# Attention values for two query halves at once, equal score pieces, and two-bank maxima

## The chip, the cores and the metric

The program runs on one core of a Trainium2 chip. The metric is the device time of one execution in microseconds (us), the median of the runs shown. TensorE (PE) multiplies, VectorE (DVE) reduces and adds, ScalarE (ACT) takes exponentials and copies, GpSimd (POOL) does small elementwise work, and SyncE (SP) issues DMAs. PEld is the weight load of TensorE, which runs beside its matmuls.

## The reference

Four layers, each a cross-attention and a feed-forward network, with the residual added around both; `x` is 8 batches of 256 tokens by 128, and the context is 8 batches of 1601 rows by 64.

```python
x = x + xattn0(layernorm(x), ctx)   # 16 heads of 8
x = x + ffn0(layernorm(x))
x = x + xattn1(layernorm(x), ctx)   # 16 heads of 64
x = x + ffn1(layernorm(x))
x = x + xattn2(layernorm(x), ctx)   # 1 head of 64
x = x + ffn2(layernorm(x))          # experts
x = x + xattn3(layernorm(x), ctx)   # 16 heads of 8
x = x + ffn3(layernorm(x))          # experts
# xattn: softmax(q k^T * scale, over 1601 keys) v, then an output product
```

## The kernel before, in words

Everything is fp32. The scheduler is told to keep the order in which the program issues (`manual_schedule`), so the order of the calls in the loops is the order in each engine's queue. PSUM, the memory that matmuls write, has eight banks of 512 columns; a stage divides them by name, as in `psum(s=4, t=2, o=1, m=1)`. A tile of a name can be written again only when the readers of the one before it in the same bank are done.

**`wide`, attentions 1 and 2.** The unit of work is a job: one batch, one head, and one half `j` of 128 queries. Attention 1 has 8 x 16 x 2 = 256 jobs, attention 2 has 16. A job holds queries on partitions and keys along the row. Its steps, with the lines that the profile names:

- `scores` (L467): four tiles `st` of 512, 512, 512 and 66 columns, each by two matmuls (the high and the low part of the queries).
- `maximum` (L474 for a tile, L477 over the four): DVE.
- `exponentials` (L488): ACT, from the score tiles into `e`, with row sums.
- `turn` (L500, copy at L502): thirteen transposes of 128 keys by PE into four `t` tiles, which ACT (the first two) and DVE (the last two) copy to `pt`.
- `values` (L514): 13 chunks of keys; even chunks write partitions 0 to 63 of the single `o` tile, odd ones 64 to 127, so that two matmuls of 64 columns of weights run side by side. They are 128 queries wide.
- `sums` (L519, L520) on DVE; `take` (L524), a copy of `o` by ACT; `project` (L528), a matmul with the output weights into the free half of `o`; `add` (L532), by DVE, to the residual.
- `query` (L438, L443, L444): once for two jobs, the queries of a later head.

The loop of job n issues: scores and maxima of n+1; turns 0 and 1 of n; project and add of n-1; the query; exponentials of n+1; turns 2 and 3 and sums of n; then values and take of n. Steps of the feed-forward networks 0 and 1, of the query weights and of the next stage are run beside the jobs by `run(beside[n], EARLY)` and `run(beside[n], LATE)`, before and after the values.

**`narrow`, attentions 0 and 3.** A unit is one batch and a group of four heads: 32 units. Keys are on partitions here, so that no transposes are needed, and the maxima are computed first, by matmuls of their own. A unit has seven steps of two chunks of 128 keys, each in two half steps t, one for each pair of heads. A half step issues: `score(p, t)` (L1069, two `st` tiles, and L1072, their exponentials on ACT); `values` (L1081) of one chunk of the step before; what is due of `beside` (keys L777, values L834, context chunks L761, queries L814, the row flip L808, the output product L913); and what is due of `tasks`: a `pair` of maxima (L873, two matmuls of 512 columns into two `pm` tiles, and L876, one DVE reduction of each) for a unit ahead, or `shift` (L882 and on), which follows the last of them. `place_shift` (L895, L897) puts the maxima into the queries. `plan` gives each `pair` a due half step, spread over a unit's fourteen, and `DONE` is the half step by which they end. The end of a unit copies the `ov` tile (L1085). Tiles: `psum(m=3, s=4, o=1)`. `bank()` hands out `st` tiles for the scores and for the work beside them. The placed keys and queries are kept for `RING = 4` units.

Of the kernel before, what the change touches and what calls it, by code (L numbers as in the profile page):

```python
# [39 lines left out]
P = 128  # L40
# [9 lines left out]
TAKEN = -3.0e38  # L50
KW = LK + 1
RING = 4
DONE = 8
AFTER = 26


# [1 line left out]
def decoder_kernel(ctx: ExitStack, tc: tile.TileContext, a: dict, out: bass.AP):  # L58
# [331 lines left out]
    def wide(layers, before, extra):  # L390
# [11 lines left out]
        with ExitStack() as es:  # L402
# [54 lines left out]
            jobs = [(k, h, j) for k in keys for h in range(layers[k[0]][0]) for j in range(QT)]  # L457
            st, e, ls, tail = {}, {}, {}, {}

            BANK = [(at, min(512, LK - at)) for at in range(0, LK, 512)]  # L460

            def scores(n, c):
                k, h, j = jobs[n]
                st[n, c] = ps["s"].tile([P, 512], F32, tag="s", name="st")
                at, w = 512 * c, min(512, KW - 512 * c)
                for i in range(2):
                    nc.tensor.matmul(st[n, c][:, 0:w], lhsT=q[k, h][i][:, j * P:(j + 1) * P],  # L467
                                     rhs=ct[k][:, at:at + w], start=(i == 0), stop=(i == 1))

            def maximum(n, c):  # L470

                if c == 0:
                    ls[n] = two.tile([P, 12], F32, tag="ls", name="ls", bufs=3)
                nc.vector.tensor_reduce(ls[n][:, c:c + 1], st[n, c][:, 0:BANK[c][1]], AX.X, ALU.max)  # L474
                if c == 3:
                    shift = ls[n][:, 4:5]
                    nc.vector.tensor_reduce(shift, ls[n][:, 0:4], AX.X, ALU.max, negate=True)  # L477
# [14 lines left out]

            def turn(n, i):

                t = ps["t"].tile([P, 512], F32, tag="t", name="t")
                p = turned[n, i] = two.tile([P, 512], F32, tag="pt", name="pt", bufs=5)
                cs = range(4 * i, min(4 * i + 4, NC))
                m = P if cs[-1] < NC - 1 else LAST
                for c in cs:
                    nc.tensor.transpose(t[0:m, (c - 4 * i) * P:(c - 4 * i + 1) * P], e[n][:, c * P:c * P + m], ident)  # L500
                w = P * len(cs)
                (nc.scalar.copy if i < 2 else nc.vector.tensor_copy)(p[0:m, 0:w], t[0:m, 0:w])  # L502

            o = {}

            def values(n, cs):

                k, h, j = jobs[n]
                if cs[0] == 0:
                    o[n] = po()  # L510
                for c in cs:
                    m = P if c < NC - 1 else LAST
                    half = slice(DC * (c % 2), DC * (c % 2) + DC)
                    nc.tensor.matmul(o[n][half, 0:P], lhsT=v[k][0:m, c, :],  # L514
                                     rhs=turned[n, c // 4][0:m, (c % 4) * P:(c % 4 + 1) * P],
                                     start=(c < 2), stop=(c >= NC - 2))
# [5 lines left out]
            def take(n):  # L522
                tail[n] = two.tile([P, P], F32, tag="os", name="os")
                nc.scalar.copy(tail[n], o[n][:, 0:P])  # L524

            def project(n):
                (l, _), h, j = jobs[n]
                nc.tensor.matmul(o[n][:, P:P + D], lhsT=tail[n], rhs=B[l][:, h, :], start=True, stop=True)  # L528

            def add(n):  # L530
                (_, b), h, j = jobs[n]
                nc.vector.scalar_tensor_tensor(X[b][:, j, :], o[n][:, P:P + D], ls[n][:, 9:10], X[b][:, j, :],  # L532
                                               ALU.mult, ALU.add)

            last = len(jobs) - 1

            loads, measures, starts, turns, ahead = {}, {}, {}, {}, {}
            for n, (k, h, j) in enumerate(jobs):
# [28 lines left out]
            for n, (_, h, j) in enumerate(jobs):  # L567
                more = n < last
                for k in loads.get(n, []):
                    load_batch(k)  # L570
                if more:
                    for c in range(4):
                        scores(n + 1, c)
                        maximum(n + 1, c)
                turn(n, 0)
                turn(n, 1)
                if n:
                    project(n - 1)
                    add(n - 1)
                for k in measures.get(n, []):  # L580
                    measure(k)
                for k in starts.get(n, []):
                    start_batch(k)
                for k in turns.get(n, []):
                    turn_y(k)

                at = n + 2 if n + 2 == first_of_last else n + 3
                if (j == 1 and n + 3 != first_of_last or at == first_of_last != n + 3) and at <= last:
                    for f in query(*jobs[at][0:2]):
                        f()  # L590
                if more:
                    exponentials(n + 1)
                turn(n, 2)
                turn(n, 3)
                sums(n)
                run(beside.get(n, []), EARLY)
                values(n, range(NC))
                take(n)
                run(beside.get(n, []), LATE)
            project(last)  # L600
            add(last)

    def maps1(two, A, B):

# [69 lines left out]
    def narrow(wq, wkT, wvT, wo, bq, bk, bv, bo, first, after=None, last=None):  # L674
# [8 lines left out]
        with ExitStack() as es:  # L683
            one = es.enter_context(tc.tile_pool(name="na1", bufs=1))
            two = es.enter_context(tc.tile_pool(name="na2", bufs=2))
            es.enter_context(psum(m=3, s=4, o=1))
            es.enter_context(tc.manual_schedule())

            def bank():
# [172 lines left out]
            def maxima(n):  # L862
# [3 lines left out]

                def pair(t, js, at, w):
                    k, q = K[n % RING][t], Q[n % RING][t]
                    pt = [pm() for g in range(2)]
                    for x, j in enumerate(js):  # L870
                        for g in range(2):
                            r = slice(64 * g, 64 * g + 64)
                            nc.tensor.matmul(pt[g][:, x * w:(x + 1) * w], lhsT=q[r, j * P:(j + 1) * P],  # L873
                                             rhs=k[r, at:at + w], start=True, stop=True)
                    for g in range(2):
                        nc.vector.tensor_reduce(mx[:, js[0]:js[-1] + 1, 2 * t + g, at // 512],  # L876
                                                pt[g][:, 0:len(js) * w].rearrange("p (j k) -> p j k", k=w),
                                                AX.X, ALU.max)

                def shift():  # L880
# [140 lines left out]
            for n in range(units):  # L1021
# [67 lines left out]

                for p in range(steps):  # L1090
                    e = two.tile([P, 4, 2, LQ], F32, tag="e", name="e")
                    for t in range(2):
                        score(p, t, e)
                        if n == p == 0:
                            spare(6)
                        if before:
                            before.pop(0)()
                        while beside and (beside[0][0] * 2 * steps < 2 * p + t + 1 or p * t == steps - 1):
                            beside.pop(0)[1]()
                        for f in tasks.pop(per * n + 2 * p + t, []):  # L1100
                            f()
                    before = [lambda c=c, e=e, values=values: values(c, e)
                              for c in range(2 * p, min(2 * p + 2, NC))]
            *inverses, project = finish(NB - 1)
# [292 lines left out]
    def ffn1(p, b):  # L1397
# [42 lines left out]

        def up(i):
            if i == 0:
                t["h"] = p.tile([P, 4, LQ], F32, name="f1_h")
# [45 lines left out]

        def take_r(j):  # L1490
            if j == 0:
                t["rT"] = p.tile([P, QT, 512], F32R, name="f1_rT")
# [441 lines left out]
```

## Time and profile before

| | us |
|---|---|
| runs | 3539.5, 3535.34, 3530.77 |
| median of the runs | 3535.34 |
| span of the profiled execution | 3529.4 |
| attention 0 | 55 to 708.5 |
| attention 1 | 737.5 to 2323 |
| attention 2 | 2323 to 2459 |
| experts of layer 2 | 2459 to 2685 |
| attention 3 | 2685 to 3318.7 |
| experts of layer 3 and output | 3318.7 to 3529.4 |

The profile is of one execution. Its page gives each engine's busy time, share of the span and number of instructions. A table by stretches gives the same by stage. The timeline lists instructions, or runs of like ones, with start, length, engine, line, operation, output and input tiles with their shapes, and, in brackets, the idle time before it with what ended it.

### The profile page before, as it was taken

Reading aid. Unit: us, or ns where it says so; the run is one execution under the profiler, and the core shown is the slowest. Engines: PE = TensorE matmul, PEld = TensorE weight load, DVE = VectorE, ACT = ScalarE, POOL = GpSimd, SP = SyncE. Lnnn points to the kernel's source line nnn. Section 1 sums busy time; section 2 is a strip of 40 time slices with the busy share of each in tenths; the row PEclk is TensorE's granted clock in tenths of the full one; section 3 lists DMA queues with packets and bytes.
Section 4 is the critical chain, followed back from the end, with each engine's and each line's share of the span. In section 5 each row is a group of like instructions: output and inputs, shape, how many; then the busy total and the mean of one; then the engine's idle time right before and its main releaser. Section 6 shows DMA issues by size and latency. Waiting matters only on the chain.

```text
span 3529.4 us, 75160 instructions
## 1 busy us (share of the span) xinstructions
PE 3380.6 (96%) x28453; PEld 2299.7 (65%) x28453; DVE 2580.6 (73%) x6482; ACT 2290.0 (65%) x5747; POOL 1179.4 (33%) x2105
## 2 busy tenths in 40 slices
PE   7999999989999999999999999988999999999999
PEld 4555555468787877788787878866445555555444
DVE  6888888656776767676776767675557888888665
ACT  3888887746666666667666666654224878787622
POOL 6344344624152513324151520131115333332100
PEclk8999999989999999999999999999998999999999
DMA  5544444120001001000100000021004444443100
GB/s 97 89 73 74 71 77 58 19 83 1 15 1 33 2 1 39 1 15 1 39 1 22 6 1 15 1 66 33 1 0 85 78 63 68 65 69 53 41 5 7
DMA packets 113449, 130.24 MB, mean 37 GB/s; under 512 B 67616, under 2 KB 96832, under 8 KB 112448
## 3 DMA queue, kind: packets, MB, share of 16 engines
q1 hardware_dynamic: 92352, 114.22, 18.0%
q0 software_dynamic: 20480, 10.53, 1.3%
q8 instruction: 225, 3.69, 0.4%
q10 hardware_dynamic: 256, 0.69, 0.1%
q14 instruction: 136, 1.11, 0.1%
HBM read 44.79 MB, written 11.28 MB: 16 GB/s over the span
## 4 chain that ended last, share of the span: by engine, by line
PE 81%; DVE 9%; ACT 6%; POOL 2%; issue 2%; DMA 0%; DVEq 0%; POOLq 0%; SPq 0%; ACTq 0%
PE ov L1081 13%; PE o L514 12%; PE st L467 12%; PE pm L873 11%; PE t L500 8%; PE st L1069 6%; PE gu L1740 3%; PE o L1789 3%; PE gu L1741 3%; ACT pt L502 3%; DVE ls L474 2%; DVE mx L876 2%; ACT e L488 2%; PE st L834 1%; DVE ql L444 1%
## 5 line engine op out<-in xcount | busy, mean ns | idle before, releaser
L876 DVE TENSOR_REDUCE mx<-pm 128x1 f32<-128x512 f32 (+1 forms) x1792 | 1020.3, 627 | 172.7 <-PE pm L873 168.9
L1072 ACT ACTIVATE e<-st 128x512 f32<-128x512 f32 (+1 forms) x1792 | 910.6, 566 | 210.5 <-PE st L1069 160.0
L474 DVE TENSOR_REDUCE ls<-st 128x1 f32<-128x512 f32 x1088 | 549.5, 567 | 292.3 <-PE st L467 291.2
L488 ACT ACTIVATE e<-st,ls 128x512 f32<-128x512 f32 x1088 | 634.0, 602 | 13.4 <-DVE ls L477 12.6
L502 ACT COPY pt<-t 128x512 f32<-128x512 f32 x544 | 293.6, 586 | 460.8 <-PE t L500 459.9
L1081 PE MATMUL ov<-e,V 128*32 128x256 f32 x6656 | 564.6, 392 | 0.3 <-ACT e L1072 0.3
L873 PE MATMUL pm<-K,Q 64*128 64x512 f32 (+1 forms) x2048 | 497.3, 451 | 18.6 <-DVE mx L876 15.4
L500 PE MATMUL t<-ident,e 128*128 128x128 f32 (+1 forms) x3536 | 506.5, 281 | 2.6
L514 PE MATMUL o<-pt,v 128*64 128x128 f32 (+1 forms) x7072 | 490.2, 278 | 17.0 <-DVE pt L502 13.0
L514 PEld LDWEIGHTS o<-pt,v 128*64 128x64 f32 (+1 forms) x7072 | 412.1, 137 | 88.2 <-DVE pt L502 37.2
L873 PEld LDWEIGHTS pm<-K,Q 64*128 64x128 f32 x2048 | 226.1, 187 | 325.8 <-DVE mx L876 223.3
L500 PEld LDWEIGHTS t<-ident,e 128*128 128x128 f32 (+1 forms) x3536 | 391.5, 141 | 52.4 <-ACT pt L502 30.0
L467 PE MATMUL st<-ct,qh 128*128 128x512 f32 x1088 | 406.1, 373 | 1.8 <-ACT e L488 1.8
L1069 PE MATMUL st<-Q,K 64*128 64x256 f32 (+1 forms) x3328 | 403.1, 287 | 0.1
L467 PE MATMUL st<-ct,ql 128*128 128x512 f32 x1088 | 362.9, 367 | 0.0
L1069 PEld LDWEIGHTS st<-Q,K 64*128 64x128 f32 (+1 forms) x3328 | 333.1, 182 | 32.3 <-issue 6.5
L855 POOL DMA_DIRECT2D Q<-qh x256 | 128.3, 501 | 450.5 <-PE st L1069 422.9
L502 DVE COPY pt<-t 128x512 f32<-128x512 f32 (+1 forms) x544 | 239.1, 481 | 34.9 <-PE t L500 34.8
L467 PEld LDWEIGHTS st<-ct,qh 128*128 128x128 f32 x1088 | 205.6, 189 | 86.3 <-issue 34.9
L1081 PEld LDWEIGHTS ov<-e,V 128*32 128x32 f32 x6656 | 142.5, 108 | 153.7 <-issue 37.9
L1742 ACT ACTIVATE act<-gu 128x512 f32<-128x512 f32 x130 | 77.5, 597 | 243.2 <-PE gu L1741 232.1
L488 ACT ACTIVATION_READ_ACCUMULATOR e<-st,ls 128x1 f32 x1088 | 230.7, 212 | 0.0
(545 smaller groups left out, 4302.2 us busy)
## 6 DMA issues: line engine op xcount, KB each, us to landing
K<-kh SPq DMA_DIRECT2D x250, 100.1 KB
K<-kl SPq DMA_DIRECT2D x250, 100.1 KB
ct<-ctd SPq DMA_DIRECT2D x23, 801.0 KB
ctd<-ct SPq DMA_DIRECT2D x8, 801.0 KB
v<-in_ctx SPq DMA_DIRECT2D x16, 384.0 KB
Q<-qh POOLq DMA_DIRECT2D x256, 16.0 KB, 2.7
Q<-ql POOLq DMA_DIRECT2D x256, 16.0 KB, 3.0
raw<-in_ctx SPq DMA_DIRECT2D x8, 384.0 KB
```

The lines of the kernel that those rows point to most:

```text
L467: nc.tensor.matmul(st[n, c][:, 0:w], lhsT=q[k, h][i][:, j * P:(j + 1) * P], rhs=ct[k][:, at:at + w], start=(i == 0), stop=(i == 1))
L474: nc.vector.tensor_reduce(ls[n][:, c:c + 1], st[n, c][:, 0:BANK[c][1]], AX.X, ALU.max)
L488: nc.scalar.activation(e[n][:, at:at + w], st[n, c][:, 0:w], AF.Exp, bias=ls[n][:, 4:5], scale=1.0, accum_out=ls[n][:, 5 + c:6 + c])
L500: nc.tensor.transpose(t[0:m, (c - 4 * i) * P:(c - 4 * i + 1) * P], e[n][:, c * P:c * P + m], ident)
L502: (nc.scalar.copy if i < 2 else nc.vector.tensor_copy)(p[0:m, 0:w], t[0:m, 0:w])
L514: nc.tensor.matmul(o[n][half, 0:P], lhsT=v[k][0:m, c, :], rhs=turned[n, c // 4][0:m, (c % 4) * P:(c % 4 + 1) * P], start=(c < 2), stop=(c ...
L855: nc.gpsimd.dma_start(out=q[r:P:8, :].bitcast(F32), in_=qhl[b][r % 2][src, :].bitcast(F32))
L873: nc.tensor.matmul(pt[g][:, x * w:(x + 1) * w], lhsT=q[r, j * P:(j + 1) * P], rhs=k[r, at:at + w], start=True, stop=True)
L876: nc.vector.tensor_reduce(mx[:, js[0]:js[-1] + 1, 2 * t + g, at // 512], pt[g][:, 0:len(js) * w].rearrange("p (j k) -> p j k", k=w), AX.X, ...
L1069: nc.tensor.matmul(st[g][0:m, j, :], lhsT=k[r, c * P:c * P + m], rhs=q[r, :], start=True, stop=True)
L1072: nc.scalar.activation(e[0:m, 2 * t + g, 0:len(cs), :], st[g][0:m, 0:len(cs), :], AF.Exp)
L1081: nc.tensor.matmul(cell["o"][32 * g:32 * g + 32, :], lhsT=v[0:m, at:at + 32], rhs=e[0:m, g, c % 2, :], start=(c == 0), stop=(c == NC - 1))
```

## The change

In `wide`, the scores are cut into four nearly equal pieces (400, 400, 400 and 401 columns, the last multiplied as 402). The turned tiles of both jobs of a pair (one batch and head, both query halves) share one `pt` buffer, and `values` multiplies a chunk for both halves at once, 256 wide; the last chunk, of 65 keys, is two matmuls of 128. In attention 1 these values are those of the pair before, half of the chunks in each job, issued after the exponentials of n+1 and before turn 2. `take` follows in the odd job, and `project` with its two adds comes at the head of the next even job, ahead of turn 0. In attention 2 the values of both jobs are issued at the odd one. In `narrow`, a pair of maxima writes one tile of two banks, which one reduction reads; scores have three banks instead of four; and a step issues the first score, the maxima due in both half steps, the second score, the work beside, and then both chunks of values. `DONE` goes from 8 to 6. Two tiles of feed-forward network 1 share a buffer.

```diff
-DONE = 8
+DONE = 6
...
-            BANK = [(at, min(512, LK - at)) for at in range(0, LK, 512)]
+            BANK = [(400 * c, 400 if c < 3 else LK - 1200) for c in range(4)]
...
-                at, w = 512 * c, min(512, KW - 512 * c)
+                at, w = BANK[c]
+                w += w % 2
...
-                    ls[n] = two.tile([P, 12], F32, tag="ls", name="ls", bufs=3)
+                    ls[n] = two.tile([P, 12], F32, tag="ls", name="ls", bufs=8)
...
-                p = turned[n, i] = two.tile([P, 512], F32, tag="pt", name="pt", bufs=5)
+                if j == 0:
+                    turned[p, i] = two.tile([P, len(cs), QT, P], F32, tag="pt" if i < 3 else "pt3", name="pt",
+                                            bufs=5 if i < 3 else 2)
...
+            HALVES = (0, 1, 2, 3, 4, 5), (6, 7, 8, 9, NC - 1, 10, 11)
...
+            def values(p, cs):
+
+                k, h, _ = jobs[QT * p]
                 if cs[0] == 0:
+                    o[p] = po()
                 for c in cs:
+                    if c == NC - 1:
+                        for j in range(QT):
+                            nc.tensor.matmul(o[p][DC * j:DC * j + DC, j * P:(j + 1) * P], lhsT=v[k][0:LAST, c, :],
+                                             rhs=turned[p, c // 4][0:LAST, 0, j, :], start=False, stop=False)
+                    else:
+                        half = slice(DC * (c % 2), DC * (c % 2) + DC)
+                        nc.tensor.matmul(o[p][half, 0:LQ], lhsT=v[k][:, c, :],
+                                         rhs=turned[p, c // 4][:, c % 4, :, :].rearrange("p j q -> p (j q)"),
+                                         start=(c < 2), stop=(c >= NC - 3))
...
+            def project(p):
+                (l, b), h, _ = jobs[QT * p]
+                for j in range(QT):
+                    nc.tensor.matmul(o[p][:, LQ + j * P:LQ + j * P + D], lhsT=tail[p][:, j * P:(j + 1) * P],
+                                     rhs=B[l][:, h, :], start=True, stop=True)
+                for j in range(QT):
+                    nc.vector.scalar_tensor_tensor(X[b][:, j, :], o[p][:, LQ + j * P:LQ + j * P + D],
+                                                   ls[QT * p + j][:, 9:10], X[b][:, j, :], ALU.mult, ALU.add)
...
+            now = layers[0][0] * NB - 1
...
+                p = n // QT
+                if j == 0 and 2 <= p <= now:
+                    project(p - 2)
                 turn(n, 0)
                 turn(n, 1)
-                if n:
-                    project(n - 1)
-                    add(n - 1)
+                if j == 0 and p > now:
+                    project(p - 1)
...
                 if more:
                     exponentials(n + 1)
+                if 1 <= p <= now:
+                    values(p - 1, HALVES[j])
+                    if j == 1:
+                        take(p - 1)
+                        if p == now:
+                            project(p - 1)
                 turn(n, 2)
                 turn(n, 3)
                 sums(n)
                 run(beside.get(n, []), EARLY)
-                values(n, range(NC))
-                take(n)
+                if p >= now and j == 1:
+                    values(p, HALVES[0] + HALVES[1])
+                    take(p)
                 run(beside.get(n, []), LATE)
...
-            es.enter_context(psum(m=3, s=4, o=1))
+            es.enter_context(psum(mm=2, s=3, o=1))
...
-                    pt = [pm() for g in range(2)]
+                    pt = ps["mm"].tile([P, 2, 512], F32, tag="mm", name="pm")
...
+                    to = mx[:, js[0]:js[-1] + 1, 2 * t:2 * t + 2, at // 512]
+                    if len(js) == 1:
+                        nc.vector.tensor_reduce(to[:, 0, :], pt[:, :, 0:w], AX.X, ALU.max)
...
+                    score(p, 0, e)
                     for t in range(2):
-                        score(p, t, e)
-                        if n == p == 0:
-                            spare(6)
-                        if before:
-                            before.pop(0)()
-                        while beside and (beside[0][0] * 2 * steps < 2 * p + t + 1 or p * t == steps - 1):
-                            beside.pop(0)[1]()
                         for f in tasks.pop(per * n + 2 * p + t, []):
                             f()
+                    score(p, 1, e)
+                    if n == p == 0:
+                        spare(6)
+                    while beside and (beside[0][0] * 2 * steps < 2 * p + 2 or p == steps - 1):
+                        beside.pop(0)[1]()
+                    for f in before:
+                        f()
```

More of the change, by code (lines that the diff above doesn't have):

```diff
@@ L493, in turn @@
             def turn(n, i):
+                p, j = divmod(n, QT)
+                cs = range(4 * i, min(4 * i + 4, NC))
                 t = ps["t"].tile([P, 512], F32, tag="t", name="t")
-                p = turned[n, i] = two.tile([P, 512], F32, tag="pt", name="pt", bufs=5)
-                cs = range(4 * i, min(4 * i + 4, NC))
+                if j == 0:
+                    turned[p, i] = two.tile([P, len(cs), QT, P], F32, tag="pt" if i < 3 else "pt3", name="pt",
+                                            bufs=5 if i < 3 else 2)
                 m = P if cs[-1] < NC - 1 else LAST
@@ L500, in turn @@
                     nc.tensor.transpose(t[0:m, (c - 4 * i) * P:(c - 4 * i + 1) * P], e[n][:, c * P:c * P + m], ident)
-                w = P * len(cs)
-                (nc.scalar.copy if i < 2 else nc.vector.tensor_copy)(p[0:m, 0:w], t[0:m, 0:w])
+                (nc.scalar.copy if i < 2 else nc.vector.tensor_copy)(
+                    turned[p, i][0:m, :, j, :], t[0:m, 0:P * len(cs)].rearrange("p (c q) -> p c q", q=P))
             o = {}
-            def values(n, cs):
-                k, h, j = jobs[n]
+            HALVES = (0, 1, 2, 3, 4, 5), (6, 7, 8, 9, NC - 1, 10, 11)
+            def values(p, cs):
+                k, h, _ = jobs[QT * p]
                 if cs[0] == 0:
-                    o[n] = po()
+                    o[p] = po()
                 for c in cs:
[L512 to L516, printed above, removed]
+                    if c == NC - 1:
[7 more added lines that the diff above has]
+                                         start=(c < 2), stop=(c >= NC - 3))
             def sums(n):
@@ L520, in sums, with take @@
                 nc.vector.reciprocal(ls[n][:, 9:10], ls[n][:, 9:10])
[L522 to L533, printed above, removed]
+            def take(p):
+                tail[p] = two.tile([P, LQ], F32, tag="os", name="os")
+                nc.scalar.copy(tail[p], o[p][:, 0:LQ])
+            def project(p):
[6 more added lines that the diff above has]
+                                                   ls[QT * p + j][:, 9:10], X[b][:, j, :], ALU.mult, ALU.add)
             last = len(jobs) - 1
+            now = layers[0][0] * NB - 1
             loads, measures, starts, turns, ahead = {}, {}, {}, {}, {}
@@ L596, in wide @@
                 run(beside.get(n, []), EARLY)
-                values(n, range(NC))
-                take(n)
+                if p >= now and j == 1:
+                    values(p, HALVES[0] + HALVES[1])
+                    take(p)
                 run(beside.get(n, []), LATE)
-            project(last)
-            add(last)
+            project(last // QT)
     def maps1(two, A, B):
@@ L872, in pair @@
                             r = slice(64 * g, 64 * g + 64)
-                            nc.tensor.matmul(pt[g][:, x * w:(x + 1) * w], lhsT=q[r, j * P:(j + 1) * P],
+                            nc.tensor.matmul(pt[:, g, x * w:(x + 1) * w], lhsT=q[r, j * P:(j + 1) * P],
                                              rhs=k[r, at:at + w], start=True, stop=True)
-                    for g in range(2):
-                        nc.vector.tensor_reduce(mx[:, js[0]:js[-1] + 1, 2 * t + g, at // 512],
-                                                pt[g][:, 0:len(js) * w].rearrange("p (j k) -> p j k", k=w),
+                    to = mx[:, js[0]:js[-1] + 1, 2 * t:2 * t + 2, at // 512]
+                    if len(js) == 1:
+                        nc.vector.tensor_reduce(to[:, 0, :], pt[:, :, 0:w], AX.X, ALU.max)
+                    else:
+                        nc.vector.tensor_reduce(to.rearrange("p j g -> p g j"),
+                                                pt[:, :, 0:len(js) * w].rearrange("p g (j k) -> p g j k", k=w),
                                                 AX.X, ALU.max)
@@ L1091, in narrow @@
                     e = two.tile([P, 4, 2, LQ], F32, tag="e", name="e")
+                    score(p, 0, e)
+                    if n == p == 0:
+                        spare(6)
                     for t in range(2):
-                        score(p, t, e)
-                        if n == p == 0:
-                            spare(6)
-                        if before:
-                            before.pop(0)()
-                        while beside and (beside[0][0] * 2 * steps < 2 * p + t + 1 or p * t == steps - 1):
-                            beside.pop(0)[1]()
                         for f in tasks.pop(per * n + 2 * p + t, []):
                             f()
+                    score(p, 1, e)
+                    if n == p == 0:
+                        spare(6)
+                    while beside and (beside[0][0] * 2 * steps < 2 * p + 2 or p == steps - 1):
+                        beside.pop(0)[1]()
+                    for f in before:
+                        f()
                     before = [lambda c=c, e=e, values=values: values(c, e)
@@ L1442, in up @@
             if i == 0:
-                t["h"] = p.tile([P, 4, LQ], F32, name="f1_h")
+                t["h"] = p.tile([P, 4, LQ], F32, tag="f1_h", name="f1_h")
             t["pt"] = pm()
@@ L1491, in take_r @@
             if j == 0:
-                t["rT"] = p.tile([P, QT, 512], F32R, name="f1_rT")
+                t["rT"] = p.tile([P, QT, 512], F32R, tag="f1_h", name="f1_rT")
             nc.scalar.activation(t["rT"][:, j, :], t["pt"], AF.Identity, bias=magic[:, 1:2], scale=1.0)
```

## The prediction

> **What bounds the kernel now.** Part 1 of the page first, then the busy time of each engine in seven stretches, cut at the first and last rows of each stage.
>
> ```profile
> PE 3380.6 (96%) x28453; PEld 2299.7 (65%) x28453; DVE 2580.6 (73%) x6482; ACT 2290.0 (65%) x5747; POOL 1179.4 (33%) x2105
> ```
>
> ```profile
> 55.00:708.50 653.50, 645.82 (x6466) 353.31 (x6465) 536.29 (x1015) 522.01 (x1084) 298.67 (x563) 0.99 0.41 66
> ...
> 737.50:2323.00 1585.50, 1520.51 (x13318) 1266.47 (x13317) 1114.96 (x3265) 1060.62 (x3192) 509.35 (x768) 1.00 0.04 12
> 2323.00:2459.00 136.00, 113.08 (x934) 93.51 (x933) 94.11 (x338) 70.22 (x200) 34.23 (x107) 0.95 0.21 58
> ...
> 2685.00:3318.70 633.70, 628.17 (x6375) 341.83 (x6374) 536.86 (x1048) 502.52 (x1034) 213.39 (x405) 1.00 0.39 61
> ```
>
> Columns: stretch, its length, then PE, PEld, DVE, ACT, POOL busy, clock, DMA. The rows are attention 0, attention 1 (256 jobs, 6.19 us each), attention 2 (16 jobs), attention 3. PE looks full everywhere, but its ends are modelled, so I go by starts. The timeline of one job of attention 1 with nothing beside it, PE and then DVE:
>
> ```profile
> 1151.31 0.50 PE L467 MATMUL st<-ct,qh 128*128 128x512 f32 x1
> ...
> 1152.94 1.09 PE L500 MATMUL t<-ident,e 128*128 128x128 f32 x8
> 1153.87 0.39 PE L528 MATMUL o<-B,os 128*128 128x128 f32 x2
> 1154.28 0.81 PE L500 MATMUL t<-ident,e 128*128 128x128 f32 x5
> 1155.02 1.75 PE L514 MATMUL o<-pt,v 128*64 128x128 f32 x26
> 1156.69 0.50 PE L467 MATMUL st<-ct,qh 128*128 128x512 f32 x1
> ```
>
> ```profile
> 1152.09 2.02 DVE L474 TENSOR_REDUCE ls<-st 128x1 f32<-128x512 f32 x4 [0.67 <-PE st L467]
> 1154.14 0.16 DVE L477 TENSOR_REDUCE ls<-ls 128x1 f32<-128x4 f32 x1
> 1154.30 0.35 DVE L532 SCALAR_TENSOR_TENSOR x<-o,ls,x 128x128 f32<-128x128 f32 x1
> 1154.97 0.89 DVE L502 COPY pt<-t 128x512 f32<-128x512 f32 x2 [0.32 <-PE t L500]
> ```
>
> 5.38 us from L467 to L467; the job before it, which also has a query (L438), takes 5.69. So a pair costs 11.07 us bare and 12.39 on average (2 x 6.19): the feed-forward steps beside it (ideally 0.67 us of PE a pair) cost 1.32. Between L528 and the second L500 PE waits 0.18 us for a t tile; the rest is work and changes of the matmul's shape. Attentions 0 and 3, in half steps, and then the end of attention 0, where no maxima are left:
>
> ```profile
> 318.65 0.55 PE L873 MATMUL pm<-K,Q 64*128 64x512 f32 x2
> 318.99 0.44 PE L1069 MATMUL st<-Q,K 64*128 64x256 f32 x4
> 319.35 0.64 PE L1081 MATMUL ov<-e,V 128*32 128x256 f32 x8
> 319.92 0.50 PE L777 MATMUL st<-ct,wkh 128*128 128x512 f32 x1
> ```
>
> ```profile
> 690.52 0.50 PE L1069 MATMUL st<-Q,K 64*128 64x256 f32 x4
> 690.95 0.64 PE L1081 MATMUL ov<-e,V 128*32 128x256 f32 x8
> ```
>
> ```profile
> 691.05 1.09 ACT L1072 ACTIVATE e<-st 128x512 f32<-128x512 f32 x2 [0.16 <-PE st L1069]
> ```
>
> Pair 0.34, scores 0.36, values 0.57: a half step is 1.27 us (318.65 to 319.92). L876 has two reductions per half step, 0.60 apart, so DVE needs 1.20 and is nearly as full as PE. A unit without extra work takes 17.78 us between its L1085 copies, a batch of four 80.0 in attention 0 and 78.9 in attention 3.
>
> **Attention 1, part by part.** Single starts in the trace give the prices. A score matmul takes 232 ns for 512 columns and 30 for 66: 0.453 ns a column, so 181 for 400. Eight of them are 1.45 us; today it is 1.63 to the first L500, with 109 ns for the first weight load after the column-split shape and 79 for the load that 66 columns can't hide. Both go. A pass of L514, two halves at once, takes 109 ns for 128 columns; a full-width matmul of 256 (L438) takes 216, so a pass of the merged values is 216. A pair of jobs has twelve of these and two of 109: 2.81 us against 2 x 1.53 now (28 issued matmul passes for 52). A change to the split shape costs 0.09 before it and 0.05 in it, the change back 0.09 and 0.055; there is still one burst a job, so these stay.
>
> Here a rule would say otherwise. The Trainium skill, TensorEngine Tiling (Array Packing), section Performance Considerations, counts some 60 cycles of overhead for each matmul; at the 2.4 GHz of TensorE: Matmul & The Clock Gate (its opening table) that is an estimated 0.6 us for 24 passes, 77 us in attention 1. The rows above (109 and 216) leave no such overhead, so I count none.
>
> Now the queues. The odd job: scores 1.45, two turns 0.93, query 0.43, switch 0.14, its half of the values 6 x 0.216 + 2 x 0.109 = 1.51, switch 0.09, turns 0.60: **5.15**. The t waits go, because 1.4 us of values stand before turn 2; the waits for DVE's pt copies go too, since these values are of the pair before.
>
> In the even job something else is late. There is one o tile. The first values of pair p-1 overwrite the one that project(p-2) fills earlier in the same job, so they wait for its two adds, and these stand in DVE's queue behind four maxima. DVE can't start the maxima when PE delivers: turns 2 and 3 of the odd job now stand at that job's very end. From the end of that job: copies and sums until 1.15 (0.09 + 1.06 by the rows at 1154.97), maxima 3 x 0.48 + 0.56, fold 0.20, adds 0.63, release 0.06: 4.04. PE gets there at 2.92 and waits 1.1 us. Then values 1.35, switch 0.09, turns 0.60: **6.08**. Bare pair 11.23: no better than 11.07.
>
> What gains is the work beside it. DVE's steps after the odd job lie on this chain (0.46 us on average), and PE's of the even job (0.30). PE's of the odd job hide behind DVE, and DVE's of the even job (0.59) mostly behind the odd job's PE. With 0.15 for normalisations and waits on ACT a pair is 12.14 against 12.39: 128 x -0.25 = **-31 us**. Bounds: if the work beside costs 1.32 as today, +20; if none of DVE's reaches the chain, 11.53 and -110. ACT keeps up: exponentials of 400 take 0.57 each from start to start, the last ends before its score tile is asked for again.
>
> **Attention 2.** Values of both jobs are issued at the odd one, so the even job waits no more for pt. It is bound by DVE and the query (8.4 us a job). Between 0 and -20; I take **-10**.
>
> **Attentions 0 and 3.** A whole step has half of the shape changes: pair 0.232, pair 0.232 and scores 0.232 follow each other in one shape, and two values cost 0.024 + 4 x 0.216 + 0.021 + 0.09 = 1.00 instead of 2 x 0.57. Unhindered: 0.34 + 0.46 + 0.23 + 0.09 + 1.00 = 2.13 us. The double reductions: by 684 ns for 512 and 289 for 132, 1.04 a column plus 0.15, so 1.22 for 1024, 1.13 from start to start, 2.27 a step for 2.40. But st has three tiles instead of four, and a step takes four: the second tile of the second score is the first one of this same step. It waits for its exponential: 690.52 to 691.05 is 0.53 after the scores start, 0.60 of ACT and 0.05 to PE: 1.18. PE is there at 0.80. Then 0.34 + 0.09 + 1.00: **2.62 us** a step. Values of the next step stand behind this wait, and so do the next scores. Five such, one of 2.05 (the 65-row chunk), one of 2.18 (one chunk of values) and place_shift at 0.30 make a unit of 17.7: as now. DVE's backlog is inside the wait. Extra work also takes st tiles and stands between scores and values. At today's price a batch is -0.25; with its own switches and waits (0.7 instead of 0.4 for a block of keys or four transposed chunks) +1.9 in attention 0, +0.1 in attention 3. That is -4 to +14 us; I take +5. Without maxima a half step costs 1.00 now (690.95 to 691.52 and the 0.43 before it), so eleven steps at the end lose some 5 us in each attention; the heads gain 1 each. Together **+13**. DONE moves the shift two half steps earlier, within this slack; the shared tile of f1_h and f1_rT orders steps that follow each other anyway.
>
> Sum: -31 - 10 + 13 = -28. The profiled execution has a span of 3529.4 us, 5.9 under the median 3535.3 of the runs, whose spread is 9; 3501 and 5.9 around it give **3508**.
>
> **Rivals.**
> A cover holds. If the third st tile is free in time, DVE's pace of 2.27 is the step, 1.15 us less a unit, 64 units: 3435. If the o tile is free in time, a pair is 5.15 + 4.95 + 1.0: 3345. For it: PE's own sums. Against it: 0.38 and 1.1 us are far above any error in these rows.
>
> Slower, by DVE. The place is the wait of the first merged values for the adds (L532) of the pair before the last. If the even job's DVE steps delay it too, a pair is 12.14 + 0.59 = 12.73, +44 us in attention 1: 3580. It decides from 0.25 of these 0.59 on. For it: DVE is in order and a late maximum makes late exponentials. Against it: about 0.9 us of room in the odd job.
>
> Nothing is left: the two waits give back just what the switches save, 3535; the change then does not unload PE, only moves where it stands.
>
> **Chances.** Forecast 0.50 (3485 to 3530, of which 0.10 within 0.3%), a cover holds 0.15, slower 0.25, nothing left 0.10. A difference of 0.3% (10.6 us) is about what a measurement of this kernel can tell from none. So faster 0.55, same 0.20, slower 0.25. Range 3430 to 3585, which leaves out the free o tile and the far end of the slower case.
>
> **What would show it.** Right: in attention 1 a row of PE's wait for L532's successor, near 1 us at every second job, odd jobs near 5.2 us; no wait of L500 for pt; in attentions 0 and 3 score blocks with their second tile 0.38 us late behind ACT, steps near 2.6 us, reductions near 1.2 us. Wrong: steps at 2.3 us or less, even jobs near 5, or merged values above 0.23 us a pass.

## The result, and the profile after

The changed kernel takes 3633.22 us (median of four runs, 3627.88 to 3636.24) against 3537.42 us for the kernel before on the same chip: a ratio of 1.0268, with a 95% interval of 1.0249 to 1.0288. It is 96 us slower; the forecast was 3508 against 3535, 27 us faster, with a range of 3430 to 3585. The profiled execution has a span of 3630.3 us, 100.9 more than that of before.

The page after, engines and then three of its costliest groups (the last column is the idle time of the engine ahead of the group, and what ended most of it):

```profile
PE 3276.5 (90%) x25189; PEld 2183.3 (60%) x25189; DVE 2478.7 (68%) x5586; ACT 2269.5 (63%) x5611; POOL 1176.7 (32%) x2105
```

```profile
L896 DVE TENSOR_REDUCE mx<-pm 128x2 f32<-128x1024 f32 x768 | 907.3, 1220 | 262.6 <-PE pm L892 258.7
L523 PE MATMUL o<-pt,v 128*64 128x256 f32 x3264 | 450.7, 399 | 154.4 <-DVE x L541 151.2
L1091 PE MATMUL st<-Q,K 64*128 64x256 f32 (+1 forms) x3328 | 534.1, 331 | 61.2 <-ACT e L1094 55.5
```

PE is busy 104 us less and DVE 102 us less, and the span grew all the same: PE's share fell from 96% to 90%. The two waits that the forecast named are both there, the merged values on the adds of DVE (L541) and the scores on ACT. The table by stretches, attentions 0, 1, 2 and 3 in this order, in the columns of the first table:

```profile
54.84:743.46 688.62, 637.77 (x6463) 366.59 (x6462) 502.68 (x581) 521.37 (x1081) 298.21 (x563) 0.98 0.42 63
773.90:2378.60 1604.70, 1424.00 (x10221) 1122.45 (x10219) 1079.69 (x3258) 1040.39 (x3063) 506.69 (x761) 0.99 0.04 12
2378.60:2534.50 155.90, 128.52 (x771) 96.47 (x770) 95.73 (x343) 69.92 (x193) 35.39 (x115) 0.85 0.18 51
2759.80:3418.20 658.40, 616.27 (x6378) 353.35 (x6378) 504.10 (x613) 501.96 (x1032) 214.51 (x405) 0.99 0.41 58
```

In attention 1 PE was busy for 1520.5 of 1585.5 us and is now busy for 1424.0 of 1604.7. Taken by its own marks (starts of score blocks, ends of units), the 100.9 us are:

| stretch | before | after | difference | forecast |
|---|---|---|---|---|
| to the end of the first unit | 85.8 | 94.6 | +8.8 | -1 |
| other 31 units of attention 0 | 622.6 | 648.9 | +26.3 | } +15 |
| other 31 units of attention 3 | 602.3 | 619.7 | +17.4 | } |
| first 255 jobs of attention 1 | 1584.6 | 1604.7 | +20.1 | -31 |
| last job of attention 1, attention 2 to its last job | 125.8 | 143.2 | +17.4 | -10 |
| last job to the first unit of attention 3 (experts between) | 268.5 | 276.8 | +8.3 | -1 |
| the rest | 239.8 | 242.5 | +2.7 | 0 |

The two rows of 31 units are not steady to the microsecond: in four other profiles with the same edits of attentions 0 and 3 and `DONE = 6` they come to +41 to +56 us together, instead of +44, and the spread lies in the last units of each attention.

A pair of jobs with nothing beside it (a bare pair) is as forecast: 5.98 us for the even and 5.14 for the odd job (medians), where 6.08 and 5.15 were expected. PE and then DVE in such an even job, which starts at 1151.10:

```profile
1152.62 0.61 PE L538 MATMUL o<-B,os 128*128 128x128 f32 x4
1153.07 1.04 PE L504 MATMUL t<-ident,e 128*128 128x128 f32 x8
1155.11 1.51 PE L523 MATMUL o<-pt,v 128*64 128x256 f32 x12 [1.00 <-DVE x L541]
```

```profile
1152.33 2.00 DVE L475 TENSOR_REDUCE ls<-st 128x1 f32<-128x400 f32 x4
1154.37 0.16 DVE L478 TENSOR_REDUCE ls<-ls 128x1 f32<-128x4 f32 x1
1154.44 0.61 DVE L541 SCALAR_TENSOR_TENSOR x<-o,ls,x 128x128 f32<-128x128 f32 x2
```

PE is done with the transposes at 1154.11 and stands until 1155.11, as the adds stand behind four maxima. What isn't as forecast is a pair with work beside it: the mean pair is 12.59 us (1604.7 / 127.5), so this work costs 1.47 us, not 0.91. A good part of the difference lies in one even job of a batch, the 11th, which grew from 6.03 to 10.07 us (mean of six batches; the first batch has no such work in it). PE in one of these, and then two windows of 5 us each, whose clock column (after the four engines and POOL) is the one to read:

```profile
1240.36 1.04 PE L504 MATMUL t<-ident,e 128*128 128x128 f32 x8
1245.01 2.83 PE L523 MATMUL o<-pt,v 128*64 128x256 f32 x12 [3.62 <-DVE x L541]
```

```profile
1240.00:1245.00 5.00, 1.40 (x13) 1.16 (x11) 4.43 (x11) 2.51 (x6) 0.00 (x0) 0.91 0.00 0
1245.00:1250.00 5.00, 4.99 (x21) 3.46 (x22) 1.04 (x5) 2.40 (x9) 0.00 (x0) 0.50 0.00 0
```

Here DVE has four convolution steps of feed-forward network 1 (L1484 and L1486, 1240.42 to 1242.3) ahead of the maxima, and these wait themselves 1.58 us for ACT's f_h (L1477), which stands behind the exponentials. So the adds come at 1244.36, PE has been idle for 3.62 us, and then works at a granted clock of 0.50: the merged values take 2.83 us instead of 1.51 (1.89 to 2.83 in the seven batches).

In attentions 0 and 3, a step after:

```profile
357.95 0.50 PE L1091 MATMUL st<-Q,K 64*128 64x256 f32 x4
358.30 0.62 PE L892 MATMUL pm<-K,Q 64*128 64x512 f32 x4
358.75 0.27 PE L1091 MATMUL st<-Q,K 64*128 64x256 f32 x1
359.20 0.50 PE L1091 MATMUL st<-Q,K 64*128 64x256 f32 x3 [0.17 <-ACT e L1094]
```

The second score (358.75) issues one matmul into the free tile; the other three wait for ACT until 359.20, 0.45 later. The column shows 0.17 idle, since a started matmul counts as busy until its modelled end. In a unit with nothing beside it a step is 0.34 + 0.46 + 0.94 + 1.00 = 2.74 us where 2.62 was forecast, and units without blocks of work take 18.43 us, not 17.7.

### The profile page after: what moved, and what is told of

It is laid out like the page before. It is cut to its first block, busy times and chain, and to the rows that moved or that the text cites. A ratio compares the mean times of both kernels' runs of the same rounds, so it can differ in the third digit from the quotient of the medians.

```text
span 3630.3 us, 67765 instructions
## 1 busy us (share of the span) xinstructions
PE 3276.5 (90%) x25189; PEld 2183.3 (60%) x25189; DVE 2478.7 (68%) x5586; ACT 2269.5 (63%) x5611; POOL 1176.7 (32%) x2105
## 4 chain that ended last, share of the span: by engine, by line
PE 65%; DVE 22%; ACT 8%; issue 3%; POOL 2%; DMA 0%; SPq 0%; ACTq 0%; POOLq 0%; DVEq 0%
PE o L523 11%; PE ov L1103 10%; PE st L1091 9%; DVE ls L475 8%; PE t L504 7%; PE st L468 6%; ACT e L1094 5%; DVE mx L896 4%; PE gu L1765 3%; PE gu L1766 3%; PE o L1814 3%; DVE pt L505 3%; PE pm L892 2%; DVE x L541 2%; PE pm L438 2%
## 5 line engine op out<-in xcount | busy, mean ns | idle before, releaser
L896 DVE TENSOR_REDUCE mx<-pm 128x2 f32<-128x1024 f32 x768 | 907.3, 1220 | 262.6 <-PE pm L892 258.7
L489 ACT ACTIVATE e<-st,ls 128x400 f32<-128x400 f32 x1088 | 634.4, 604 | 74.6 <-DVE ls L478 71.1
L523 PE MATMUL o<-pt,v 128*64 128x256 f32 x3264 | 450.7, 399 | 154.4 <-DVE x L541 151.2
L1091 PE MATMUL st<-Q,K 64*128 64x256 f32 (+1 forms) x3328 | 534.1, 331 | 61.2 <-ACT e L1094 55.5
L475 DVE TENSOR_REDUCE ls<-st 128x1 f32<-128x400 f32 x1088 | 546.3, 564 | 29.1 <-PE st L468 28.5
L1103 PE MATMUL ov<-e,V 128*32 128x256 f32 x6656 | 457.3, 389 | 0.0
L468 PE MATMUL st<-ct,qh 128*128 128x400 f32 x1088 | 420.9, 387 | 4.9 <-ACT e L489 4.2
L523 PEld LDWEIGHTS o<-pt,v 128*64 128x64 f32 x3264 | 212.3, 140 | 295.3 <-DVE x L541 181.1
L468 PE MATMUL st<-ct,ql 128*128 128x400 f32 x1088 | 380.5, 350 | 0.0
L892 PE MATMUL pm<-K,Q 64*128 64x512 f32 (+1 forms) x2048 | 321.1, 381 | 29.7 <-DVE mx L896 21.4
L1103 PEld LDWEIGHTS ov<-e,V 128*32 128x32 f32 x6656 | 171.9, 109 | 143.2 <-issue 42.4
```

The costliest lines, as they stand in the source:

```text
L523: nc.tensor.matmul(o[p][half, 0:LQ], lhsT=v[k][:, c, :], rhs=turned[p, c // 4][:, c % 4, :, :].rearrange("p j q -> p (j q)"), start=(c < 2 ...
L892: nc.tensor.matmul(pt[:, g, x * w:(x + 1) * w], lhsT=q[r, j * P:(j + 1) * P], rhs=k[r, at:at + w], start=True, stop=True)
L896: nc.vector.tensor_reduce(to[:, 0, :], pt[:, :, 0:w], AX.X, ALU.max)
L1091: nc.tensor.matmul(st[g][0:m, j, :], lhsT=k[r, c * P:c * P + m], rhs=q[r, :], start=True, stop=True)
L1103: nc.tensor.matmul(cell["o"][32 * g:32 * g + 32, :], lhsT=v[0:m, at:at + 32], rhs=e[0:m, g, c % 2, :], start=(c == 0), stop=(c == NC - 1))
```

## The experiments

All runs are timed against the kernel before on the same chip; the ratio has its 95% interval behind it. A difference from the changed kernel compares different chips, on which the kernel before took 3537 to 3542 us. The first two take the change apart.

**Attentions 1 and 2 alone** (the hunks of `wide`, and the shared tile of f1_h and f1_rT).

> Only the edits in attentions 1 and 2; attentions 0 and 3 as before. Theory (the loss adds up stage by stage): attention 1 costs 20 us and attention 2 some 17 to 19 more than before, nothing else changes, so 3537 + 39 = 3576. Rival (the two halves of the change harm each other, by the clock or by what lies between the stages): well away from 3576, below 3560 or above 3592.

Measured: 3568.82 us, 1.0082 (1.0065 to 1.0100). Attention 1 takes 1603.2 and the stretch after it 141.5, within 2 us of the changed kernel; the units of attentions 0 and 3 take 622.6 and 602.3, as before.

**Attentions 0 and 3 alone** (the hunks of `narrow`, and `DONE = 6`).

> Only the edits in attentions 0 and 3 (with DONE 6); attentions 1 and 2 as before. Theory: the first unit +9 in attention 0, the other units +26 and +17, and +6 up to the first unit of attention 3: 3537 + 60 = 3597. Rival (my prediction's +13, the rest being an effect of the other half): 3550.

Measured: 3596.46 us, 1.0160 (1.0141 to 1.0179). The two halves, 28 and 56 us, make 84 of the 96: they add up within the intervals, and the larger loss is the one that I took for a small one.

**The adds earlier.** In `wide`, `project` is split into its matmuls and its adds, and both move up:

```diff
...
                     for c in range(4):
                         scores(n + 1, c)
+                        if c == 2 and j == 0 and 2 <= p <= now:
+                            project(p - 2)
+                    for c in range(4):
                         maximum(n + 1, c)
+                        if c == 1 and j == 0 and 2 <= p <= now:
+                            add(p - 2)
...
-                if j == 0 and 2 <= p <= now:
-                    project(p - 2)
...
```

> The changed kernel, but the project of the pair before the last is issued after the third score of the even job and its two adds after the second maximum instead of after the fold. Theory (PE's wait for the adds is what attention 1 pays): the wait of 1.0 us in each of 127 even jobs goes, even jobs near 5.0 us, and the long stalls of the even jobs with feed-forward steps shorten too: 3633 - 130 to - 170, so 3465 to 3505. Rival (DVE is the bound: the adds put in front delay the last maxima, and so the exponentials, by 0.6 us): even jobs stay near 6 us, and the time stays within 20 us of 3633.

Measured: 3527.27 us, 0.9969 (0.9956 to 0.9982) of the kernel before, 106 less than the changed kernel. Attention 1 falls from 1604.7 to 1505.4 us. PE in a bare even job, and then the first row of PE's waits in attention 1, for the changed kernel and for this one (us in total, times, longest):

```profile
1236.87 1.04 PE L504 MATMUL t<-ident,e 128*128 128x128 f32 x8
1237.84 1.51 PE L523 MATMUL o<-pt,v 128*64 128x256 f32 x12
```

```profile
PE o L523 <- DVE x L541: 151.2, 126, 3.8
```

```profile
PE o L523 <- DVE x L544: 36.7, 38, 2.4
```

The bare even job is 4.94 us instead of 5.98, and the wait is left only in jobs with much DVE work beside them. This wait, not the merging, is what attention 1 pays for. In the even job the maxima that the adds delay are covered. The gain stays short of the 130 us expected: 37 us of the wait remain in jobs with DVE work, and the odd job of some pairs is longer (bare 5.52 at the median for 5.14), so that part of what the even job gains comes back there.

**Attention 2 with values of each job alone**, 128 wide, in both jobs of a pair:

```diff
-                if p >= now and j == 1:
+                if p == now and j == 1:
                     values(p, HALVES[0] + HALVES[1])
                     take(p)
+                if p > now:
+                    values_one(n)
+                    if j == 1:
+                        take(p)
...
```

> The changed kernel, but attention 2 multiplies values 128 wide in each job, as before the change. Theory (values of both jobs at the odd one stand behind the batch's query there, with nothing to cover the even job): attention 2 goes back from 143 to some 126 to 130 us, 3633 - 15 = 3618. Rival (the chain from one batch's residual to the next one's query sets attention 2, and the order of the values means nothing): 3633.

Measured: 3624.75 us, 1.0239 (1.0221 to 1.0256), 8 us less than the changed kernel, which the intervals barely tell apart; the profile is clearer. The stretch goes from 143.2 to 133.0 us, short of the 126 to 130 expected. What is left of the 17.4 is the last job of attention 1: 14.5 us in both, 7.66 before. It holds the second half of one pair's values, their copy, product and adds, and then the whole values of the next pair, all in the one `o` tile; no run takes this crossing apart. What the late values do in attention 2, by PE in its first odd job, in the changed kernel:

```profile
2400.25 0.38 PE L257 MATMUL pm<-ident,ln_y 128*128 128x128 f32 x2
2403.78 0.70 PE L438 MATMUL pm<-yT,A 128*128 128x256 f32 x2 [3.15 <-DVE yT L260]
```

The next batch's query waits for a copy behind DVE's maxima, 0.84 us in this job before, 3.15 now: the even job, with no values in it, is over in 4.1 us, so PE comes to the query early and DVE doesn't. After that PE has both halves' values to do, 4 us in one piece. The granted clock in the stretch is 0.85, before it was 0.95.

**Two-bank maxima and three score tiles alone**, in half steps, DONE 8 (the change's hunks of `psum` and `pair` on the kernel before).

> The kernel before, with two-bank maxima and three score tiles alone: half steps, DONE 8, attentions 1 and 2 as before. Theory (the loss comes from asking for four score tiles in one step where there are three): a half step asks for two, the third is free, units within 0.3 us of 17.78, so 3540 + 0 to 10, most of it at the end of attention 0. Rival (three score tiles are too few in any order): units of 18.4 us or more, 3580 or more.

Measured: 3519.5 us, 0.9937 (0.9919 to 0.9955), 22 less than before. Bare units go from 17.78 to 17.67, those with other work by up to 0.8 less in attention 3. Three score tiles are enough where a half step asks for two; the shorter reductions are a gain.

**Whole steps alone**, one-bank maxima, four score tiles, DONE 8 (the change's hunk of the step loop).

> The kernel before, with whole steps alone: one-bank maxima, four score tiles, DONE 8, attentions 1 and 2 as before. Theory (the same): with four score tiles no score waits within the step, the four reductions of 0.60 us set a step at 2.4 us, a unit 17.0 us, 3540 - 40 = 3500. Rival (the order itself is bad: work beside and values late, DVE idle at the start of each step): units of 18 us or more, 3560 or more.

Measured: 3791.43 us, 1.0705 (1.0669 to 1.0741), on the rival's side, and far beyond what either gave. PE's first wait in attention 0 after its first unit:

```profile
PE pm L873 <- DVE mx L876: 103.6, 177, 1.0
```

A whole step asks for four maxima tiles and there are three: the fourth matmul waits 0.55 us for a reduction, and then PE does scores and values before it brings the next pair, while DVE, done with its three, is idle for 0.65 to 0.8. A step is 0.65 + 2.48 = 3.13 and more. In the changed kernel two double tiles hold a step's pairs, so this is another wait than the one that I looked for, and says nothing of that.

**DONE 8** in the edits of attentions 0 and 3.

> The edits of attentions 0 and 3 with DONE 8 instead of 6. Theory (in the first unit all fourteen pairs of the next unit are due in DONE half steps, and DVE sets it): the first unit goes from 94.3 to about 90 and the first of attention 3 likewise; 3596 - 6 = 3590. Rival (the first unit is late by the order and the tiles): 3596, first unit 94.

Measured: 3591.54 us, 1.0144 (1.0125 to 1.0162), by the total not told apart from DONE 6. By the profile the first unit ends at 88.3 instead of 94.3, and the stretch to the first unit of attention 3 is 270.9 instead of 275.6. With 6, the fourteen pairs for the next unit fall due in six half steps of the first one.

**One chunk of values between the maxima and the second score** (with DONE 8):

```diff
                         for f in tasks.pop(per * n + 2 * p + t, []):
                             f()
+                    if before:
+                        before.pop(0)()
                     score(p, 1, e)
```

> As the run with DONE 8, but one chunk of the values of the step before is issued ahead of the second score of a step, the other after the work beside. Theory (PE waits 0.45 us a step for ACT to free the third score tile): 0.57 us of values cover this wait, one more change of shape costs 0.1; a step of 2.74 becomes 2.4, a unit 18.4 becomes 16.5 to 17, 64 units: 3590 - 100 = 3490. Rival (DVE or ACT sets the step, the wait only shows it): units stay above 18, 3580.

Measured: 3610.59 us, 1.0195 (1.0172 to 1.0219): 19 worse than without it, bare units 19.1. By its prices this speaks against my theory; the waits of scores for ACT did fall, from 52.0 us to 30.8 in the whole run. But the changes of shape are four in a step again (0.34 + 0.67 + 0.57 + 0.43 + 0.57 = 2.58), and the second score, now later, is too near to the next step's first, which waits for the third tile in its place. The run can't tell the theories apart; the next one was made for that.

**Short exponentials** (with DONE 8). ACT takes the exponentials of 64 of each 256 queries and leaves out the rest, and the values read these four times:

```diff
-                        nc.scalar.activation(e[0:m, 2 * t + g, 0:len(cs), :], st[g][0:m, 0:len(cs), :], AF.Exp)
+                        nc.scalar.activation(e[0:m, 2 * t + g, 0:len(cs), 0:64], st[g][0:m, 0:len(cs), 0:64], AF.Exp)
...
-                                         rhs=e[0:m, g, c % 2, :], start=(c == 0), stop=(c == NC - 1))
+                                         rhs=e[0:m, g, c % 2, None, 0:64].to_broadcast([m, 4, 64]), start=(c == 0), stop=(c == NC - 1))
```

> As the run of the edits of attentions 0 and 3 with DONE 8, but the exponentials take only the first 64 of each 256 queries, and the values use these four times; the other scores are left out, PE's work stays the same. Theory (PE waits for ACT to free the third score tile): the wait of 0.45 us in a step goes, then DVE's 2.3 to 2.4 us set it, units of 16.3 to 17 us instead of 18.4: 3592 - 90 to - 130, so 3460 to 3500. Rival (the bunched order itself, DVE idle at the head of each step, sets the step): units above 18, 3570 or more.

Measured: 3469.32 us, 0.9800 (0.9782 to 0.9818), 122 less than the same kernel with whole exponentials. Bare units are 16.96 us. A step, PE:

```profile
358.35 0.51 PE L1072 MATMUL st<-Q,K 64*128 64x256 f32 x4
358.69 0.99 PE L873 MATMUL pm<-K,Q 64*128 64x512 f32 x4
359.52 0.40 PE L1072 MATMUL st<-Q,K 64*128 64x256 f32 x4
359.85 1.07 PE L1084 MATMUL ov<-e,V 128*32 128x256 f32 x16
```

DVE beside it, without a gap:

```profile
356.77 6.08 DVE L877 TENSOR_REDUCE mx<-pm 128x2 f32<-128x1024 f32 x5 [0.43 <-PE pm L873]
```

The second score is whole again, and a step is 2.35 to 2.5 us: the pace of DVE, as the forecast had it (2.27) for a free tile. So the wait for ACT's exponentials in the third score tile is the price of whole steps: 1.5 us in a bare unit (18.5 with DONE 8, now 16.96) and up to 2.6 in units with other work (21.7, now 19.1). The edit unloads ACT everywhere, so not all of the 122 us need be this one wait.

**Equal pieces alone** (the hunk of `BANK` on the kernel before).

> The kernel before, with the four equal score pieces alone. Theory (PE sets a job of attention 1, and the 66-column piece costs it a weight load that it can't hide): 0.18 us in each of 272 jobs, 3541 - 45 = 3496. Rival (DVE's and ACT's row from maximum to exponential sets the job): within 10 us of 3541.

Measured: 3510.43 us, 0.9917 (0.9895 to 0.9940). This is 28 us less, of 45 expected: the theory's side, but not its size. Bare jobs are 0.13 us shorter (5.40 to 5.27, 5.71 to 5.58) and attention 1 takes 22.0 us less. If the parts add up, which no run shows for this one, the pieces give 22 within the change too, and all else in attention 1 costs 42.

**Two feed-forward steps a job later**, from the end of an odd job to the end of an even one:

```diff
-    F1_AT = (3, 5, 7, 8, 9, 10, 13, 14, 15, 16, 26)
+    F1_AT = (3, 5, 7, 8, 10, 11, 13, 14, 15, 16, 26)
```

> The changed kernel, with two steps of feed-forward network 1 (the second half of the first product with its convolution, and the tanh after it) one job later, so that the convolution's DVE work stands at the end of an even job, ahead of the odd job's maxima, instead of the other way. Theory (DVE work at the end of an odd job lies on the chain maxima, adds, merged values; at the end of an even job it is covered): the job of 10 us in each batch falls to 6 to 6.5 us, the next grows by up to 0.7: 3633 - 20 to -25 = 3610. Rival (ACT's order, the convolution behind the exponentials, delays it in any place): 3633.

Measured: 3613.06 us, 1.0204 (1.0181 to 1.0227), 20 less than the changed kernel. The 11th job falls from 10.07 to 6.69 us, the one before it from 7.05 to 6.35, and the next grows from 5.59 to 6.30: together 3.4 us a batch less for the same two steps, and attention 1 falls from 1604.7 to 1579.2. What counts is whether the maxima behind DVE's part are those that the adds wait for; PE's part of the first product moves with it, and no run moves DVE's alone.

**The parts that gain, together**: attention 1 with early adds, attention 2 as in its run, attentions 0 and 3 with half steps, two-bank maxima, three score tiles, DONE 8.

> Attention 1 with the early adds, attention 2 with values 128 wide in each job, attentions 0 and 3 in half steps with two-bank maxima, three score tiles and DONE 8. Theory (the parts add up): attention 1 -80 against the kernel before, attention 2 and what follows +10, attentions 0 and 3 -22: 3541 - 92 = 3450. Rival (the parts meet in the same engines, part of the gain is lost): 3475 to 3520.

Measured: 3439.0 us, 0.9718 (0.9696 to 0.9740), 99 less than the kernel before and 194 less than the changed one. Attention 1 takes 1502.3 us, units in attentions 0 and 3 are as with two-bank maxima alone, PE is busy for 95% of the span. The parts add up (3450 was expected).

## Why the prediction was wrong

- **Attention 1, bare: right.** Pieces of 400 columns, passes of 0.216, two split shapes a pair, and the wait for the adds (1.0 us, forecast 1.1; 126 waits, 151.2 us) came out within 0.1 us a job. The early adds show that the wait was the cause and not a symptom.
- **Attention 1, work beside: the failed step.** "PE's of the odd job hide behind DVE, and DVE's of the even job (0.59) mostly behind the odd job's PE", and DVE's after the odd job were put at their mean busy time, 0.46. The term was sized at 0.91 us (0.46 + 0.30 + 0.15) and is 1.47: 0.56 x 127.5 = 71 us, less 14 by which the bare pair (11.12 for 11.23) is better. By the starts in the changed kernel's trace, averaged over 125 pairs, the work costs in three places. From the odd job's last transpose to the merged values it is 4.76 us for 4.04 bare (4.04 was forecast): 0.72 for the 0.46. From there to the end of the even job it is 2.43 for 1.97: 0.46 for the 0.30 of PE's work. The odd job up to its last transpose is 5.38 for 5.11: 0.27 that the forecast had hidden, save for the 0.15 of normalisations and waits on ACT.
  A step of several engines isn't late by its busy time. In the 11th job the maxima begin 3.96 us after its first score (1238.28 to 1242.24), against 1.23 in the bare job (1151.10 to 1152.33). Of these 2.7 us the convolution is busy for 1.9, which the mean of 0.46 contains; the rest is its wait for ACT, which is behind its exponentials, and the lower clock adds up to 1.3 to the merged values. Without the 11th jobs the 4.76 is 4.59. The shift by one job takes most of its 4 us away (25 us in attention 1). The other 45 or so of the 71, PE's work after the merged values and in the odd job above all, no run takes apart.
  The upper bound that the forecast gave (1.32 "as today, +20") has the right total by luck: the work costs more than this bound, and the better bare pair made up for it. Its rival "Slower, by DVE" named the place, in attention 1 alone.
- **Attention 2: wrong sign.** "The even job waits no more for pt" is true, but its values were the cover for DVE's chain to the next query. +10.5 us for that, given back by 128-wide values in each job; the crossing from one scheme to the other in the last job of attention 1, +6.9, was put at nothing without a reason: it was not in the sum at all, and its cause stays untested.
- **Attentions 0 and 3: right mechanism, too small.** The wait for the third tile was put at 0.38 and is 0.45 (released at 1.25 us from the step's start, not 1.18), and the score cut into 1 + 3 matmuls takes 0.49 after it, not 0.43, I take it because two halves that run side by side are parted. 0.12 us x 5 steps x 62 units = 37 us, which covers the 29 between the +15 forecast and the +44 measured; the short exponentials confirm the cause. (The rival's 1.15 us a unit for a free tile is too little by the forecast's own steps: 5 x (2.62 - 2.27) is 1.75. The short exponentials gave 1.5.)
- **DONE and the first units: open.** "Within this slack" leaves out the first units, where nothing was planned ahead. By one pair of profiles DONE 6 costs 6.0 us there in attention 0 and 4.7 at the start of attention 3, but the total doesn't show it. The other profiles don't agree either: the stretch to the first unit of attention 3, 268.5 before, is 272.6 with equal pieces alone and 275.5 with attentions 1 and 2 alone, both with DONE 8, and the first unit of attention 0 ends at 93.2 with DONE 8 and short exponentials. So most of the 17 us of these stretches stays unplaced.
- **Parts that gain alone.** Equal pieces (28 us) and two-bank maxima in half steps (22 us) gain on the kernel before. In the forecast they stand inside steps that the waits lengthen; how much of each is left within the change no run shows. The rival "a cover holds" had a pair at 5.15 + 4.95 + 1.0 = 11.1 us for an o tile free in time. With the early adds the bare even job is 4.94, as it says, but the bare odd job is 5.52 and the mean pair 11.8 (1505.4 / 127.5).

## What to carry to other kernels

When values are moved a pair later, look at who frees the tile that they write: here an add that stood behind four maxima on DVE cost 100 us, and two calls moved up in the issue order gave it back. Work beside a loop is priced at the chain that its slowest engine stands on, job by job, not at its mean busy time; the same two steps cost 3.4 us less a batch when they stood one job later. Merging steps of a pipeline halves the changes of shape, but it also asks for all buffers of a step at once: count tiles per step before counting switches.

## What the runs showed of the hardware

A wait of PE costs more than its length when it is long. After 3.62 us idle the granted clock was 0.50 in the next 5 us, and twelve merged values took 2.83 us instead of 1.51; after the 1.0 us waits of the bare jobs nothing of this is seen. The Trainium skill, TensorE: Matmul & The Clock Gate, section Part 1: The HAM clock gate, has the clock halved after an idle window of about 3.4 us, which fits these rows. Here a shorter wait can be followed by it too:

```profile
2215.69 1.70 PE L523 MATMUL o<-pt,v 128*64 128x256 f32 x12 [2.17 <-DVE x L541]
2217.00:2220.00 3.00, 3.00 (x12) 2.68 (x11) 1.50 (x5) 0.58 (x3) 0.96 (x2) 0.50 0.00 0
```

A wait of 2.00 us at 2229.35 has the same behind it, while seven others of 2.10 to 2.12 us in attention 1 left the merged values at 1.51 to 1.52. No run here separates what the clock alone cost. In attention 1 its mean is 0.99 against 1.00 before, an estimated 16 us of 1605; attention 2, whose seven waits for its queries were up to 3.1 us long, ran at a mean clock of 0.85 against 0.95 before.

The idle column of a group can be far below what a wait costs. In the step of the changed kernel above, it shows 0.17 us where the second matmul starts 0.45 after the first. With DONE 8, scores waited 52.0 us for ACT by that column; with the short exponentials it was 5.6, and the kernel was 122 us faster, though not all of this need be the wait.
